# Attention and a mixture of experts on 4096 tokens: the results of three quarters of the tokens are summed and stored while experts still run

## The chip, the cores and the metric

The kernel runs on one core of one Trainium2 chip, as one launch. A core has five engines that run their own instruction streams side by side and wait for one another by semaphores: TensorE (PE in the profile, with its weight loads as PEld), VectorE (DVE), ScalarE (ACT), GpSimd (POOL) and SyncE (SP, which here only issues DMAs and reads small numbers). DMAs are issued into queues by SP, ACT and POOL and move data between DRAM and on-chip memory. The metric is the time of one execution in device microseconds (us); lower is better.

## The reference

The input is 16 sequences of 256 tokens with 128 channels, 4096 tokens in all. Cut to what matters:

```python
xn  = layernorm(x)
# attention: 16 heads of 8 channels, causal
Q, K, V = relu(xn @ Wq + bq), relu(xn @ Wk + bk), relu(xn @ Wv + bv)
attn = softmax(causal(Q @ K.T / sqrt(8)))          # per head
o    = attn @ V + xn
att  = gamma * (o - mean(o)) / sqrt(var(o) + eps) + beta
# mixture of experts: 8 experts, each token goes to its best two
h     = rms_weight * xn * rsqrt(mean(xn * xn) + eps)
top_w, top_i = top_k(softmax(h @ gate_w.T), 2)     # weights scaled to sum 1
moe   = xn + sum over the two: top_w * (silu(h @ w1.T) * (h @ w3.T)) @ w2.T   # 448 inner
out   = x + att + moe
```

Each of the eight experts has three matrices of 448 by 128. A token's result needs its attention and the results of two experts, whichever these are.

## The kernel before, in words

The 4096 tokens are 32 groups of 128 (one token per partition), in 8 blocks of 4 groups (`NB`, `BT`, 512 tokens: two sequences). Attention runs in 16 units, two per block: a unit `(n, r)` is block n with one half of the heads. Its parts are called `scores` (the products of queries and keys `S`, then VectorE's row maxima `tops`, lines 663 to 694), `queries` (`Qs`, `Qm`, line 705 on), `weights` (`W` and the exponentials `e`, lines 739 to 765, with causal masks on GpSimd), `values` (`O`, lines 780 and 791) and `finish` (transposes `o_ps`, `y`, and the statistics `mv`, lines 804 to 847).

Tokens are routed in three parts, `ROUTES`: groups 0 to 15, 16 to 23 and 24 to 31. `route` writes each token's row and weight into a DRAM list of its expert (GpSimd indirect DMAs, line 555). `planned` (line 856) turns the number of tokens per expert into a plan: which 256 rows of which expert each tile works on. The tiles come in three waves (9 possible after the first part, 17 after the second, the rest after the third; `WAVES`), and the plan goes through a wave expert by expert. 36 tiles are the usual count (`USUAL`); the up to three more stand behind a branch on the real count (line 1225).

`experts` (line 942) handles one tile after another. A tile is fetched two tiles ahead on SP's queue (its 256 rows `frows` and the three matrices, with 5, 3, 3 and 2 buffers), its rows are transposed (`hT`), and two halves of `A` and `G` (line 1000) give `hid` by way of ACT (line 1008) and VectorE (lines 1009 and 1011); `Y` (line 1017) is the down product. `deliver` transposes it back (`R_ps`, line 1031), adds the rows' own share on VectorE (`fres`, line 1033), and GpSimd scatters the rows with two indirect DMAs into `places`, a DRAM array with two rows for every token (line 1037). So a token's two expert results lie side by side in `places` once both of its tiles are delivered.

`rest` (line 1079) completes a pair of blocks on the attention side: SP loads x (line 1084, one buffer), GpSimd adds beta and x into `xn` (lines 1086, 1087), VectorE does a Newton square root on the statistics (`lv` at line 1090, `newton_sqrt` at 261 to 273, `nm` at line 1093), ACT scales `y` (line 1099), GpSimd multiplies by gamma and adds `xn` (lines 1100, 1101).

The order of TensorE's instructions is the order in which the program is written. Between the parts of a unit the program calls `fill` (line 1133), seven times per unit: each call adds an allowance for routing and planning, for exact masks and for the experts (1.57 expert steps, `EXPERT_STEPS`; a tile has four steps) and lets that much of each go on, and one step of `rest`. The other engines' orders, SP's and POOL's queues among them, are decided by a scheduler, which takes what is ready by its own reckoning of times; so an operation may stand far from its place in the program.

At the end, when all tiles are delivered, eight loads of 512 KB bring `places` back, one per block (`z`, line 1238, alternately in SP's and ACT's queue), VectorE adds the two rows to `y` (16 additions, line 1243), and eight stores of 256 KB write the output (line 1244):

## Time and profile before

| | |
|---|---|
| median of 10 runs | 701.37 us (699.7 to 703.02) |
| the profiled execution's own time | 702.03 us |
| its span in the profile | 700.1 us |
| TensorE busy, mean granted clock | 555.6 us (79%), 0.909 |
| VectorE / ScalarE / GpSimd busy | 470.6 / 321.4 / 271.7 us |
| DMA | 50.81 MB, mean 73 GB/s |
| 72 scatters of expert results (line 1037) | 72.4 us of GpSimd |
| 16 additions of `z` (line 1243) | from 684.0 us on; median 0.685 us of one |

Times in the profile count from the start of the span. The slices show in tenths how busy an engine was in each fortieth of the span (17.5 us). "PEclk" is the clock that TensorE was granted, 1.00 being full speed. In the time line a row is: start, length, engine, line, operation, output and inputs with their shape, and in brackets how long the engine stood idle before it and what it then waited for. The chain of waits is followed back from the last instruction; its rows are: start, length, what.

### The profile page before, as it was taken

The numbers are of one execution on the slowest core, as the hardware profiler recorded it, in microseconds if no ns is written. First come the engines' busy times: TensorE is split into PE (matmuls) and PEld (weight loads), VectorE is DVE, ScalarE is ACT, GpSimd is POOL, SyncE is SP. The second block draws the span as 40 slices with busy tenths as digits, with TensorE's granted clock in tenths as the row PEclk, the third lists the DMA queues.
The fourth block names the chain that finished last, engine by engine and source line by source line (L and its number), as shares of the span: only waits on it lengthen the run. The fifth ranks groups of instructions, "written<-read, shape, count | busy, mean of one in ns | idle before, by whom it ended". The sixth has DMA issues, their size and how long they took to land.

```text
span 700.1 us, 10306 instructions
## 1 busy us (share of the span) xinstructions
PE 555.6 (79%) x3280; PEld 330.9 (47%) x3293; DVE 470.6 (67%) x1287; ACT 321.4 (46%) x708; POOL 271.7 (39%) x401
## 2 busy tenths in 40 slices
PE   0267879597898919989799999889999998999830
PEld 0133434243565506555456555555566555556520
DVE  4956799854477934969558676968377649674356
ACT  2353466238434624354354545384454452835420
POOL 7600006880001572116733325264224235773451
PEclk9988879759899959999899999999999999999975
DMA  6000001115112322223332312332132312331019
GB/s 166 1 0 1 0 1 35 42 39 156 45 44 63 86 78 63 62 58 116 103 110 68 95 56 62 93 95 68 49 95 61 95 58 63 116 116 53 16 47 327
DMA packets 40760, 50.81 MB, mean 73 GB/s; under 512 B 5924, under 2 KB 33072, under 8 KB 40704
## 3 DMA queue, kind: packets, MB, share of 16 engines
q1 hardware_dynamic: 32128, 38.11, 18.6%
q0 software_dynamic: 4352, 8.47, 3.7%
q10 hardware_dynamic: 4224, 3.55, 1.6%
q8 instruction: 27, 0.44, 0.3%
q14 instruction: 29, 0.24, 0.1%
HBM read 38.35 MB, written 12.27 MB: 72 GB/s over the span
## 4 chain that ended last, share of the span: by engine, by line
PE 55%; DVE 26%; ACT 11%; DMA 4%; issue 2%; another core or an unknown queue 1%; POOL 0%; SPq 0%; DVEq 0%; ACTq 0%; POOLq 0%
PE S L663 8%; PE A L1000 8%; PE Y L1017 8%; PE G L1000 7%; PE W L739 6%; ACT e L762 4%; PE S L676 4%; PE O L780 4%; DVE tops L686 3%; DVE tops L694 3%; PE O L791 2%; PE q_ps L600 2%; ACT p L419 2%; DMA y<-in_x_dram 2%; DMA z<-places 2%
## 5 line engine op out<-in xcount | busy, mean ns | idle before, releaser
L1037 POOL DMA_INDIRECT places<-fres,frows x72 | 72.4, 1005 | 219.2 <-DVE fres L1033 149.3
L762 ACT ACTIVATE e<-W 128x512 f32<-128x512 f32 x192 | 99.9, 602 | 56.7 <-PE W L739 29.3
L1009 DVE SCALAR_TENSOR_TENSOR th<-th,A 112x512 f32<-112x512 f32 x72 | 49.2, 684 | 99.1 <-ACT th L1008 89.0
L694 DVE TENSOR_REDUCE tops<-S 128x2 f32<-128x512 f32 x128 | 79.6, 681 | 29.7 <-PE S L676 26.3
L1000 PE MATMUL A<-hT,w 128*112 128x256 f32 x288 | 78.8, 397 | 15.1 <-ACT hT L991 11.3
L765 POOL TENSOR_SCALAR_AFFINE_SELECT e<-e 128x256 f32<-128x256 f32 (+1 forms) x108 | 51.0, 496 | 79.2 <-ACT e L762 77.3
L663 PE MATMUL S<-KTm,QT 32*128 32x256 f32 (+1 forms) x512 | 76.9, 566 | 1.5 <-ACT e L762 1.5
L1000 PE MATMUL G<-hT,w 128*112 128x256 f32 x288 | 77.2, 392 | 0.0
L1017 PE MATMUL Y<-hid,w 112*128 112x256 f32 x288 | 72.2, 395 | 4.5 <-DVE Qs L712 2.1
L555 POOL DMA_INDIRECT lists<-rows_c,ratu_c x64 | 66.3, 1037 | 18.6 <-issue 16.7
L739 PE MATMUL W<-Qm,KT 32*128 32x512 f32 (+1 forms) x512 | 62.6, 544 | 3.0 <-ACT Qm L715 3.0
L1000 PEld LDWEIGHTS A<-hT,w 128*112 128x112 f32 x288 | 48.9, 182 | 33.2 <-ACT hT L991 14.9
L1017 PEld LDWEIGHTS Y<-hid,w 112*128 112x128 f32 x288 | 55.4, 197 | 18.7 <-issue 3.5
L1000 PEld LDWEIGHTS G<-hT,w 128*112 128x112 f32 x288 | 52.8, 183 | 12.2
L1008 ACT ACTIVATE th<-A 112x512 f32<-112x512 f32 x72 | 43.0, 597 | 32.7 <-PE A L1000 31.9
L801 ACT COPY oT<-O 128x512 f32<-128x512 f32 x32 | 18.7, 585 | 78.4 <-PE O L791 64.9
L1011 DVE TENSOR_TENSOR hid<-th,G 112x512 f32<-112x512 f32 x72 | 49.3, 685 | 7.4 <-PE O L791 1.7
L663 PEld LDWEIGHTS S<-KTm,QT 32*128 32x128 f32 x512 | 35.7, 200 | 22.1 <-issue 10.3
L780 PE MATMUL O<-e,vstat 128*32 128x512 f32 x256 | 39.0, 661 | 7.8 <-DVE Qs L712 4.4
L600 PE MATMUL q_ps<-xnT,wq_sb 128*128 128x512 f32 x32 | 22.4, 787 | 28.5 <-DVE Qs L712 22.7
L686 DVE TENSOR_REDUCE tops<-S 128x4 f32<-128x512 f32 x64 | 39.8, 681 | 4.6 <-PE S L676 4.5
L676 PE MATMUL S<-cmask,ident_bf 128*128 128x256 bf16 (+1 forms) x192 | 39.2, 330 | 0.0
(238 smaller groups left out, 860.3 us busy)
## 6 DMA issues: line engine op xcount, KB each, us to landing
w<-in_w1T_dram SPq DMA_DIRECT2D x36, 224.0 KB
w<-in_w3T_dram SPq DMA_DIRECT2D x36, 224.0 KB
w<-in_w2T_dram SPq DMA_DIRECT2D x36, 224.0 KB
frows<-lists SPq DMA_DIRECT2D x36, 130.0 KB
x<-in_x_dram SPq DMA_DIRECT2D x8, 256.0 KB
z<-places SPq DMA_DIRECT2D x4, 512.0 KB
z<-places ACTq DMA_DIRECT2D x4, 512.0 KB
lists<-filling SPq DMA_DIRECT2D x9, 130.0 KB
```

Of the source, the lines that this page charges most:

```text
L555: ins = G.indirect_dma_start(out=lists, out_offset=bass.IndirectOffsetOnAxis(ap=at_u[:, r, b + t : b + t + 1], axis=0), in_=rows[:, t, :], ...
L663: T.matmul(out, lhsT=QT[rows, q0 : q0 + P], rhs=KTm[rows, :, b * SEQ : b * SEQ + nk], start=(part < 2 or b == 0), stop=False, skip_group_c ...
L676: T.matmul(out, lhsT=ident_bf, rhs=cmask[:, 0, :].unsqueeze(1).to_broadcast([P, 4 if part == 2 else 2, P]), start=False, stop=True, skip_g ...
L686: ins = V.tensor_reduce(top[:, :, 0, cols], sp[g].rearrange("p (b j k) -> p b j k", b=2, j=HG), AX.X, ALU.max, negate=True,).ins
L694: ins = V.tensor_reduce(top[:, part, 1, cols], sp[g].rearrange("p (j k) -> p j k", j=HG), AX.X, ALU.max, negate=True,).ins
L739: T.matmul(out, lhsT=KT[rows, k0 : k0 + P], rhs=Qm[rows, :, k0 : (b + 1) * SEQ], start=(part > 0 or b == 0), stop=on_pool and (part > 0 or ...
L762: ins = S.activation(e[:, g, :], sp[g], AF.Exp).ins
L765: behind["POOL"] = G.affine_select(on, on, [[0, nd], [1, P]], ALU.is_ge, no_weight, base=0, channel_multiplier=-1).ins
L780: T.matmul(op[rows, :], lhsT=v[:, 2 * b, r * NG + g, :], rhs=e0[:, g, :], start=True, stop=False, skip_group_check=True, tile_position=(0, ...
L1000: T.matmul(to[:, ts(c, SL)], lhsT=wt[:, 0, ts(2 * k + c, CI)], rhs=hT, start=True, stop=True,)
L1017: T.matmul(yp, lhsT=w2[:, 0, c, :], rhs=hid[c // 2][:, ts(c % 2, SL)], start=(c == 0), stop=(c == NCI - 1),)
L1037: ins = G.indirect_dma_start(out=places, out_offset=bass.IndirectOffsetOnAxis(ap=rows[:, a, C : C + 1].bitcast(U32), axis=0), in_=res[:, a ...
```

## The change

`sums(pool, blocks)` takes the place of the final loop. For each block it loads `z` on SP, adds the two rows of `z` to each other and then adds `y` (two VectorE operations of 512 elements, into `z`), and stores `z` on SP. Loads run four blocks ahead of the additions (`LAG`), with six buffers in memory that the routing's pool has given back. It is called by `early_sums` from `fill` and from the last experts: blocks 0 to 3 begin once tile 26 is delivered in program order and the attention side of these blocks is complete, blocks 4 and 5 once tile 33 is (`READY`). Blocks 6 and 7 follow behind all experts.

This holds if the tiles that the first 16 groups need are among the first 26 in the plan, and those of the first 24 groups among the first 33. `planned` now orders a wave's tiles in turns over the experts (first tile of every expert, then the second, and so on) instead of expert by expert. It puts the pairs of expert and tile on partitions and gets each one's number from small TensorE products. The last wave's plan also counts the tiles that stand too late; if there are any, the sums and stores of blocks 0 to 5 are repeated at the very end, behind a branch.

`rest` for blocks 4 and 5 moves from behind all units into the last block's units. `EXPERT_STEPS` goes from 1.57 to 1.56. The DMAs that fill the lists' ends stand in another group of independent writes.

```diff
-    FIRST_US, EARLY_US, MASK_US, EXPERT_STEPS, EXPERTS_FROM = 4.0, 1.1, 0.7, 1.57, 3
+    FIRST_US, EARLY_US, MASK_US, EXPERT_STEPS, EXPERTS_FROM = 4.0, 1.1, 0.7, 1.56, 3
+    READY = [(16, 26), (24, 33)]
...
     def planned(w):
...
-        before = tiny("before", [P, E])
-        pair = norm.tile([P, E, E], F32, tag="pair", name=f"pair_{w}")
-        V.tensor_tensor(pair, earlier, left.unsqueeze(1).to_broadcast([P, E, E]), ALU.mult)
-        V.tensor_reduce(before, pair, AX.X, ALU.add)
...
+        there = tiny("there", [P, 1], BF16)
+        V.tensor_tensor(there, by_pair[:, 0:1], pair_j, ALU.is_gt)
...
+        yield PAUSE
+        op = misc(f"order_ps_{w}")[:, 0:1]
+        T.matmul(op, lhsT=behind_bf, rhs=there, start=True, stop=False)
+        T.matmul(op, lhsT=ones_bf, rhs=there, start=False, stop=True)
+        number = tiny("number", [P, 1])
+        V.scalar_tensor_tensor(number, there, -FAR, op, ALU.mult, ALU.add)
...
+        chosen = tiny("chosen", [P, 2, nk])
+        for k, of in ((0, pair_e), (1, row)):
+            V.tensor_scalar(
+                chosen[:, k, :], tile_no[:, 0:nk], number, of, ALU.is_equal, ALU.mult
+            )
...
+        yield PAUSE
+        cp = misc(f"plan_ps_{w}")[:, : 2 * nk]
+        T.matmul(
+            cp, lhsT=ones_f, rhs=chosen.rearrange("p a k -> p (a k)"), start=True, stop=True
+        )
...
+            wp = misc(f"worked_ps_{w}")[:, 0:E]
+            T.matmul(wp, lhsT=ones_bf, rhs=done, start=True, stop=True)
...
+        lp = misc(f"late_ps_{w}")[:, 0:NR2]
+        T.matmul(lp, lhsT=ones_bf, rhs=late_bf, start=True, stop=True)
+        late_i = tiny("late_i", [P, 1], I32)
+        V.tensor_reduce(late_i, lp, AX.X, ALU.max)
+        tiles_at["late"] = late_i
...
+    def sums(pool, blocks):
+        at = {}
+        for k in range(len(blocks) + LAG + 1):
+            if 0 <= k - LAG - 1 < len(blocks):
+                n = blocks[k - LAG - 1]
+                nc.sync.dma_start(out=ov[:, ts(n, BT), :], in_=at.pop(n)[:, :, 0, :])
+            if k < len(blocks):
+                n = blocks[k]
+                z = pool.tile([P, BT, 2, C], F32, tag="z", bufs=ZBUFS, name=f"z_{n}")
+                ins = nc.sync.dma_start(out=z, in_=pv[:, ts(n, BT)]).ins
+                tc.add_to_no_dep_group("places", ins)
+                at[n] = z
+            if 0 <= k - LAG < len(blocks):
+                n = blocks[k - LAG]
+                z = at[n]
+                V.tensor_tensor(z[:, :, 0, :], z[:, :, 0, :], z[:, :, 1, :], ALU.add)
+                V.tensor_tensor(z[:, :, 0, :], z[:, :, 0, :], y[:, ts(n, BT), :], ALU.add)
+            yield
+    LAG, ZBUFS = 4, 6
...
         beside(side["rest"])
+        early_sums()
+    last_pool = []
+    def early_sums():
+        if not last_pool:
+            if delivered[0] <= READY[0][1] or exact_upto[0] < NB or rested[0] < READY[0][0] // BT:
+                return
+            assert next(early_work, None) is None
+            early.__exit__(None, None, None)
+            last_pool.append(tc.tile_pool(name="last", bufs=1))
+            last_pool.append(last_pool[0].__enter__())
+            side["sums"] = sums(last_pool[1], range(READY[0][0] // BT))
+        if delivered[0] > READY[1][1] and rested[0] >= READY[1][0] // BT and not summed:
+            summed.append(True)
+            side["sums"] = chain(
+                side["sums"], sums(last_pool[1], range(READY[0][0] // BT, READY[1][0] // BT))
+            )
+        next(side["sums"], None)
...
-        if r == 0 and n % 2 == 0 and n >= 4:
+        if r == 0 and n in (4, 6, 7):
             for _ in side["rest"]:
                 pass
-            side["rest"] = rest(n - 4, n - 2, ffn_pool)
+            k = {4: 0, 6: 2, 7: 4}[n]
+            side["rest"] = rest(k, k + 2, ffn_pool)
...
-    side["rest"] = chain(rest(NB - 4, NB - 2, ffn_pool), rest(NB - 2, NB, ffn_pool))
+    side["rest"] = rest(NB - 2, NB, ffn_pool)
     for _ in side["experts"]:
         next(side["rest"], None)
+        early_sums()
...
-    early.__exit__(None, None, None)
-    late_pool.__exit__(None, None, None)
-    last = ctx.enter_context(tc.tile_pool(name="last", bufs=NB, reuse_waits="tile"))
-    for n in range(NB):
-        z = last.tile([P, BT, 2, C], F32, tag="z", name=f"z_{n}")
-        eng = nc.sync if n % 2 == 0 else nc.scalar
-        eng.dma_start(out=z, in_=pv[:, ts(n, BT)])
-        zs.append(z)
-    for n in range(NB):
-        yn = y[:, ts(n, BT), :]
-        for r in range(2):
-            V.tensor_tensor(yn, yn, zs[n][:, :, r, :], ALU.add)
-        (nc.sync if n % 2 == 0 else nc.scalar).dma_start(out=ov[:, ts(n, BT), :], in_=yn)
+    while len(summed) < 1:
+        early_sums()
+    for _ in side["sums"]:
+        pass
+    for _ in sums(last_pool[1], range(READY[1][0] // BT, NB)):
+        pass
+    with tc.If(number("late", P) > 0):
+        for _ in sums(last_pool[1], range(READY[1][0] // BT)):
+            pass
+    last_pool[0].__exit__(None, None, None)
```

## The prediction

> **What bounds the kernel now.** I read the page's busy table, slices and chain by engine first:
>
> ```profile
> span 700.1 us, 10306 instructions
> PE 555.6 (79%) x3280; PEld 330.9 (47%) x3293; DVE 470.6 (67%) x1287; ACT 321.4 (46%) x708; POOL 271.7 (39%) x401
> PE   0267879597898919989799999889999998999830
> DMA  6000001115112322223332312332132312331019
> PE 55%; DVE 26%; ACT 11%; DMA 4%; issue 2%; another core or an unknown queue 1%; POOL 0%; SPq 0%; DVEq 0%; ACTq 0%; POOLq 0%
> ```
>
> TensorE carries the kernel until the last two slices (8, 3, then 0); in the last one DMA is at 9. So an end without TensorE can be shortened, while in the middle whatever holds TensorE up costs its full length. Second, busy time by stretch (stretch, length, PE, PEld, DVE, ACT, POOL, granted clock, DMA share, GB/s), here 605 to 640 us and two pieces of the end:
>
> ```profile
> 605.00:640.00 35.00, 33.54 (x222) 20.78 (x218) 22.63 (x46) 18.41 (x39) 21.55 (x27) 1.00 0.31 89
> 665.00:680.00 15.00, 6.10 (x40) 3.95 (x32) 9.69 (x33) 3.29 (x8) 6.49 (x6) 0.84 0.05 16
> 680.00:700.00 20.00, 0.00 (x0) 0.00 (x0) 11.00 (x16) 1.64 (x5) 5.43 (x4) 0.50 0.92 315
> ```
>
> At 605 to 640 TensorE idles 1.5 us of 35, VectorE 12: extra VectorE work fits there only if TensorE need not wait for what stands behind it. After 680 DMA is 92% busy. Third, the chain of waits and the time line at the end:
>
> ```profile
> 677.15 2.13 DMA places<-fres,frows
> 679.49 4.38 DMA z<-places
> 686.92 6.17 DMA z<-places
> 695.75 0.69 DVE y L1243
> ...
> 678.02 0.17 DVE L1093 SCALAR_TENSOR_TENSOR nm<-mv,l_r 128x8 f32<-128x8 f32 x1
> 684.08 1.69 POOL L1101 TENSOR_TENSOR y<-y,xn 128x512 f32<-128x512 f32 x1
> 693.22 3.23 DVE L1243 TENSOR_TENSOR y<-y,z 128x512 f32<-128x512 f32 x5 [1.41 <-DMA z<-places]
> ```
>
> The last scatter's start releases eight loads of 512 KB 2.13 us later; they last until about 693, though `y` itself is complete at 684.08 + 1.69 = 685.8. Fourth, the time line at 577 to 586, the one place where VectorE, GpSimd and an x load collide late in the kernel, and its clock:
>
> ```profile
> 577.47 4.27 DVE L625 TENSOR_SCALAR KTm<-KT,head_mask 128x512 f32<-128x512 f32 x1
> 577.71 2.51 POOL L1086 TENSOR_TENSOR xn<-xn,beta_sb 128x512 f32<-128x512 f32 x2
> 582.74 1.88 PE L1000 MATMUL A<-hT,w 128*112 128x256 f32 x4 [1.81 <-DVE th L1009]
> 584.32 1.26 POOL L1087 TENSOR_TENSOR xn<-xn,x 128x512 f32<-128x512 f32 x1 [2.88 <-DMA x<-in_x_dram]
> ...
> 584.00:586.00 2.00, 2.00 (x6) 1.22 (x4) 1.86 (x7) 0.00 (x0) 1.26 (x1) 0.50 0.21 61
> ```
>
> A KTm that usually takes 0.48 lasts 4.27 us while GpSimd does beta and x adds. TensorE idles 1.81, and the granted clock then reads 0.50: the A and G groups take 1.88 and 1.91 instead of 1.03. That is 1.81 + 0.85 + 0.88 = 3.5 us for one VectorE delay of 3.8.
>
> **1. The tail.** Removed behind the last scatter: six of eight z loads, twelve of sixteen adds, six of eight stores; scatter-to-sum no longer sets the end. Next late is the normalising chain of the last eight groups. Before, `nm` ends at 678.2 and the last GpSimd operation at 685.8, that is nm + 7.6 (eight scales on ACT, then four GpSimd operations of 1.26 to 1.69). In the new order the last attention transposes stand one A/G group earlier on TensorE (before: "A1_35, o_ps, R34"; after: "o_ps, A1_35, R34"), worth 1.75, so the first tiny operation (`lv`) starts near 670.5 instead of 671.7. Its chain took 6.5 us and now shares VectorE with z4's and z5's four adds (0.70 each, 2.8): nm at 679.8. GpSimd ends at 687.4; one last add 0.7, issue 0.45, store to end 3.2 (before: 696.9 to 700.1), and a branch on the late flag, 0.3 (the scales of `y` on ACT around before's count branch took 1.50 for three instead of 0.43 each): 692.0. Against 700.1 that is -8.1. z6 and z7 are issued near 680 behind the last scatter and, at the 4.38 of the first z load above, land near 685.5, before `y`; if loads needed that row's 6.17 they would still tie. Unshown is how a z add beside GpSimd's operations stretches (one add took 1.64 instead of 0.69): 0 to 2.5 us more.
>
> **2. Sums among the experts.** z0 to z3: 2 MB of loads, eight adds, four stores, moved into 605 to 640. On SP the z loads wait for the scatters of tiles 28 and 29, and the fetches of 33 and 34 queue behind them; those are two tiles ahead of use (a tile takes about 9 us here), so a delay of 3 us is covered; without that cover a late tile costs its full delay. The outs wait on SP for the adds, with frows_34 and weights of 33 behind them, again under the same cover. VectorE has no cover. The four adds of z0, z1 stand ahead of the row maxima `tops` of the last unit's first scores, of fres29 and of tile 30's second half. Placed on the trace by hand: fres28 at 606.1, its scatter landed at 609.6, z0 and z1 landed near 613.1 (3.5 for 512 KB, between 2.85 of a 256 KB x load and 4.38); VectorE is ready at 610.4, ends the adds at 615.9 and `tops` at 618.4, and TensorE's weights of that unit start 2.8 late. For z2 the same count gives 3.7 late; z3 is landed by then. Stores add nothing to VectorE. Bounds: 0, if loads land before VectorE arrives, and 6.5 of idle plus twice 1.7 of slow clock, 9.9. The nearest row is the KTm block: a VectorE delay of 3.8 cost 3.5. Two such: I take +7.0.
>
> [...]
>
> **3. The rest work moved.** x adds and normalising of blocks 4 and 5 go from the end to the last block's units, those of 2 and 3 stand elsewhere against KTm. In the new GpSimd order beta and x adds of blocks 2 and 3 no longer lie where KTm of the last block runs, by a gap near 576.7 to 579.5 that it just fits: -3.5 (bounds -3.5 and 0). GpSimd now waits for block 5's x load, one buffer, ahead of a causal mask of the last unit: before, such a wait was 2.88 and 2.67 us; the mask has over 2 us of slack behind the late `tops` of step 2: +0.5 (0 to 2). The 17 tiny VectorE operations of the moved normalising (0.2 each, 3.5) leave the same engine earlier: 0 beside work that waits anyway, at worst 3.5 if `Qs` stands behind them.
>
> **4. Planning.** VectorE's planning instructions go from 74 to 66 of about 0.2 us, beside other work: 0, at worst 1.6 less or more. TensorE gets some 12 tiny matmuls, nearest the logit ones (64 in 8.2 us, 0.13 each): +1.6. They wait for VectorE with a pause between, which leaves whole work steps of cover; uncovered, a wait is one VectorE operation. The new tile order is the same 36 tiles of equal size: 0. EXPERT_STEPS 1.56 moves experts half a step later, already counted in 1. Counted with the inputs, the last tile that first-half tokens need is number 23 (of 26 allowed), and 31 (of 33) for the third quarter: the late flag stays 0 and the repetition does not run.
>
> Sum: -8.1 + 7.0 - 3.5 + 0.5 + 1.6 = **-2.5**. The profiled execution, 702.03 (its span 700.1 and 1.9 around it), is 0.66 above the median 701.37; from the median: **698.9**.
>
> **Rivals.**
> A, slower: one mechanism, the z adds at the head of VectorE's queue. If both waits come in full with the slow clock (9.9) and KTm is still stretched (0 for -3.5): -8.1 + 9.9 + 0.5 + 1.6 = +3.9, 705.3. It decides from the point where the waits cost over 6.0 with KTm unhelped, or 9.5 with it. For it: TensorE idles only 1.5 of 35 us there. Against: the last three tiles end with TensorE waiting on chains anyway, which can absorb some.
> B, loads hidden: the DMA share is 0.31 at 605 to 640, so z lands early and the waits cost 1: -8.1 + 1 - 3.5 + 0.5 + 1.6 = -8.5, 692.9. Against: a scatter-to-sum path of 7 us, and VectorE reaches the adds before.
> C, the tail keeps half: the z adds and GpSimd hold each other up, as in the KTm row, and the tail gains 4 only: +1.6, 703.0. Against: two tiny chains interleaved leave gaps.
> D, the repetition runs after all: 6 x 768 KB = 4.5 MB at the tail's 315 GB/s, about 15 us, with its own tail saved none: near 714. Only a wrong count would do it.
>
> **How the numbers follow.** My forecast .36, A .32, B .20, C .11, D .01. The trace also holds one TensorE idle stretch of 13.9 us (before 259.8) whose releaser the profile doesn't name; it can move with the order, which widens each case by a few us. The range reaches from under B, 690, to just past A, 706. About 0.2% (1.4 us) is what the measurement can tell from no change. Faster by more than that: B, most of the forecast, a little of C: .52. Within: .11. Slower: A, the rest of C, D: .37.
>
> **What would show it.** Step 1: one or two z loads behind the last scatter, end set by POOL's last `y` add, TensorE's last matmul to the span's end near 19 us instead of 27. Step 2: adds on VectorE at 610 to 630 with idle ended by "DMA z" of 2 to 4 us, PE idle before the last unit's W, and a granted clock below 1 behind it. Step 3: KTm of the last block at 0.5. Step 4: no second set of z loads. By the sum TensorE's last matmul ends near 678.3 (672.7 + 5.6); I am wrong if it ends before 675 or after 682.

## The result, and the profile after

| | before | after |
|---|---|---|
| median | 700.88 us of 40 runs (698.19 to 703.19) | 713.98 us of 11 runs (712.54 to 719.91) |
| profiled execution, its span | 702.03, 700.1 | 716.78, 714.5 |
| ratio of the times, 95% interval | | 1.0196 (1.018 to 1.0212) |

The changed kernel is 2.0% slower by the ratio of the times; the two medians alone give 1.9%. The forecast was 698.9 with a range of 690 to 706: wrong in sign, and the result lies outside the range. The profiled execution of after is 2.8 us above its median, that of before 1.1, so the spans below differ by 14.4 us where the medians differ by 13.1. The page of the changed kernel, the lines shown of before:

```profile
span 714.5 us, 10340 instructions
PE 568.6 (80%) x3295; PEld 337.5 (47%) x3308; DVE 457.1 (64%) x1279; ACT 322.0 (45%) x708; POOL 274.9 (38%) x403
PE   0267888497897867957999999989998999988870
DMA  6000001114112221222422321423223214353123
PE 54%; DVE 22%; ACT 12%; issue 5%; DMA 3%; another core or an unknown queue 2%; POOL 2%; DVEq 0%; POOLq 0%; ACTq 0%; SPq 0%
```

TensorE is busy 13 us longer for nearly the same work, and its slices 13 to 21 hold 7, 8, 6, 7, 9, 5, 7, 9, 9, where before has a single slice of 1 (the idle stretch of 13.9 us) and 7 to 9 otherwise. The end has lost the slice in which DMA is busy for 90% or more (9 before, 3 now). To see where the time went I cut both spans at the starts of attention's transposes `o_ps`, of which there are 32, one for each sequence and half of the heads:

| stage, cut at the n-th `o_ps` | before | after | difference |
|---|---|---|---|
| start to 8th | 218.3 | 221.2 | +2.9 |
| 8th to 14th (planning, list scatters) | 134.8 | 149.8 | **+15.0** |
| 14th to 26th | 215.1 | 210.1 | -5.0 |
| 26th to 28th (KTm of the last block) | 39.9 | 34.8 | -5.1 |
| 28th to 32nd (last unit, early sums) | 59.9 | 72.9 | **+13.0** |
| 32nd to the end | 32.2 | 25.7 | -6.5 |

Busy time by stretch (stretch, length, PE, PEld, DVE, ACT, POOL, granted clock, DMA share, GB/s): the two stages in bold, first of before, then of after, and of after the 35 us around the sums and the end too:

```profile
218.29:353.09 134.80, 108.81 (x660) 66.50 (x661) 92.09 (x261) 58.23 (x127) 57.28 (x72) 0.91 0.27 81
608.00:667.85 59.85, 56.09 (x349) 36.29 (x349) 31.80 (x71) 27.97 (x57) 30.42 (x42) 0.97 0.19 57
```

```profile
221.24:371.03 149.79, 117.25 (x670) 72.40 (x671) 89.73 (x252) 58.38 (x127) 59.43 (x72) 0.90 0.25 74
615.95:688.82 72.87, 62.84 (x350) 39.42 (x350) 40.17 (x97) 29.37 (x59) 36.89 (x47) 0.91 0.33 103
616.00:651.00 35.00, 31.41 (x169) 19.29 (x168) 24.26 (x57) 10.90 (x21) 13.94 (x17) 0.85 0.48 151
695.00:714.00 19.00, 0.18 (x2) 0.00 (x0) 8.47 (x23) 3.19 (x8) 9.31 (x8) 0.53 0.38 120
```

In the last unit TensorE runs the same 350 matmuls; it idles 10.0 us instead of 3.8 and is busy 6.8 longer at a lower granted clock (0.91 instead of 0.97). The planning stage is different: there VectorE does less than before, TensorE has ten more matmuls, and yet it idles 32.5 us instead of 26.0 and is busy 8.4 longer.

The time line of after around the first sums (start, length, engine, line, operation, and in brackets the idle time ahead of it and what ended it):

```profile
624.16 1.11 DVE L1193 TENSOR_TENSOR z<-z 128x512 f32<-128x512 f32 x1 [2.40 <-POOL e L771]
627.62 2.48 DVE L700 TENSOR_REDUCE tops<-S 128x2 f32<-128x512 f32 x4
628.36 3.86 PE L745 MATMUL W<-Qm,KT 32*128 32x512 f32 x8 [3.24 <-DVE tops L700]
632.15 2.05 PE L1066 MATMUL A<-hT,w 128*112 128x256 f32 x4
638.57 0.69 DVE L1193 TENSOR_TENSOR z<-z 128x512 f32<-128x512 f32 x1 [1.94 <-DMA z<-places]
```

This is step 2's picture: four additions ahead of `tops`, TensorE idle for 3.24 us before `W`, and then `W`, `A` at a granted clock of 0.50 from 628.4 to 634.2 (3.86 and 2.05 us; 1.14 and 1.03 before). The end of after, by the chain of waits (start, length, what) and by the time line:

```profile
698.91 2.44 DMA places<-fres,frows
701.42 3.68 DMA z<-places
705.12 1.48 DVE z L1193
706.72 1.54 DVE z L1194
```

```profile
694.75 0.44 PE L1097 MATMUL R_ps<-ident,yT 128*128 128x128 f32 x2 [0.52 <-DVE z L1193]
700.29 0.17 DVE L1160 SCALAR_TENSOR_TENSOR nm<-mv,l_r 128x8 f32<-128x8 f32 x1
706.12 1.59 POOL L1168 TENSOR_TENSOR y<-y,xn 128x512 f32<-128x512 f32 x1
709.00 0.69 DVE L1194 TENSOR_TENSOR z<-z,y 128x512 f32<-128x512 f32 x1
```

Two z loads are left behind the last scatter. They land at 705.1, before `y` is complete at 707.7, and TensorE's last matmul ends 19.3 us before the end: step 1 as forecast. The stretched KTm is gone; in after the last two blocks' KTm on VectorE read:

```profile
580.32 0.49 DVE L631 TENSOR_SCALAR KTm<-KT,head_mask 128x512 f32<-128x512 f32 x1 [2.79 <-issue]
591.25 0.47 DVE L631 TENSOR_SCALAR KTm<-KT,head_mask 128x512 f32<-128x512 f32 x1
```

What the prediction has no step for is the planning stage. At 306 to 327 us of after:

```profile
314.83 0.86 PE L797 MATMUL O<-e,vstat 128*32 128x256 f32 x8
325.31 0.58 ACT L807 COPY oT<-O 128x512 f32<-128x512 f32 x1 [9.45 <-remote]
325.95 0.69 PE L1097 MATMUL R_ps<-ident,yT 128*128 128x128 f32 x2 [9.89 <-issue]
```

ACT copies `O`, whose last matmul is recorded as ended at 315.7, only at 325.31. Its idle time is put down to "remote", that is, to no releaser that the profile shows. The 13.9 us stretch of before that the prediction named is of the same kind: VectorE waits 5.5 and 3.8 us for products that TensorE had long written (`o_ps` and `top_ps` are recorded as ended at 245.4 and 245.9), and TensorE's next instruction waits for `Qs`, which comes of the second. (TensorE's own row names `Qs`; it is VectorE's waits that have no releaser.)

```profile
254.82 0.17 DVE L813 TENSOR_SCALAR rs<-o_ps 128x16 f32<-128x16 f32 x1 [5.50 <-remote]
259.06 0.69 DVE L712 TENSOR_TENSOR Qs<-QT,top_ps 128x512 f32<-128x512 f32 x1 [3.77 <-remote]
259.80 2.08 PE L600 MATMUL q_ps<-xnT,wq_sb 128*128 128x512 f32 x2 [13.91 <-DVE Qs L712]
```

I call these late completions: a consumer starts late, in these two profiles 2 to 13 us after the recorded end of the matmul it needs, and the profile shows no releaser. All whose wait is over 2.5 us begin to wait within bursts of the routing's list scatters (`lists`, GpSimd: before 108 to 159, 240 to 262, 324 to 347; after 109 to 159, 246 to 269, 309 to 331). ACT and VectorE idle 20.7 us for "remote" in before, and ACT 27.2 in after; not all late completions are put down so, and the sum is no measure of what they cost.

One sentence of the description of the kernel has to be put right: `fres` does not add the rows' own share; it multiplies the tile's result by the router's weight.

### The profile page after: what moved, and what is told of

Its sections match the earlier page's. It is cut to its first block, busy times and chain, and to the rows that moved or that the text cites. A ratio compares the mean times of both kernels' runs of the same rounds, so it can differ in the third digit from the quotient of the medians.

```text
span 714.5 us, 10340 instructions
## 1 busy us (share of the span) xinstructions
PE 568.6 (80%) x3295; PEld 337.5 (47%) x3308; DVE 457.1 (64%) x1279; ACT 322.0 (45%) x708; POOL 274.9 (38%) x403
## 4 chain that ended last, share of the span: by engine, by line
PE 54%; DVE 22%; ACT 12%; issue 5%; DMA 3%; another core or an unknown queue 2%; POOL 2%; DVEq 0%; POOLq 0%; ACTq 0%; SPq 0%
PE Y L1083 8%; PE A L1066 7%; PE S L669 7%; PE G L1066 6%; PE W L745 6%; PE O L786 4%; ACT e L768 4%; PE S L682 4%; DVE tops L700 4%; PE O L797 2%; PE q_ps L606 2%; DVE tops L692 2%; DMA y<-in_x_dram 2%; ACT p L422 1%
## 5 line engine op out<-in xcount | busy, mean ns | idle before, releaser
L1103 POOL DMA_INDIRECT places<-fres,frows x72 | 73.9, 1026 | 226.2 <-DVE fres L1099 172.4
L1083 PE MATMUL Y<-hid,w 112*128 112x256 f32 x288 | 76.0, 409 | 16.3 <-DVE taken L517 4.6
L745 PE MATMUL W<-Qm,KT 32*128 32x512 f32 (+1 forms) x512 | 65.8, 559 | 5.7 <-DVE tops L700 3.2
L786 PE MATMUL O<-e,vstat 128*32 128x512 f32 x256 | 40.5, 676 | 7.7 <-DVE rs L827 7.2
L692 DVE TENSOR_REDUCE tops<-S 128x4 f32<-128x512 f32 x64 | 39.9, 681 | 5.4 <-PE S L682 5.4
L1091 ACT COPY yT<-Y 128x256 f32<-128x256 f32 x36 | 13.4, 372 | 57.8 <-PE Y L1083 57.7
```

Source lines behind the costliest of these rows:

```text
L692: ins = V.tensor_reduce(top[:, :, 0, cols], sp[g].rearrange("p (b j k) -> p b j k", b=2, j=HG), AX.X, ALU.max, negate=True,).ins
L745: T.matmul(out, lhsT=KT[rows, k0 : k0 + P], rhs=Qm[rows, :, k0 : (b + 1) * SEQ], start=(part > 0 or b == 0), stop=on_pool and (part > 0 or ...
L786: T.matmul(op[rows, :], lhsT=v[:, 2 * b, r * NG + g, :], rhs=e0[:, g, :], start=True, stop=False, skip_group_check=True, tile_position=(0, ...
L1083: T.matmul(yp, lhsT=w2[:, 0, c, :], rhs=hid[c // 2][:, ts(c % 2, SL)], start=(c == 0), stop=(c == NCI - 1),)
L1103: ins = G.indirect_dma_start(out=places, out_offset=bass.IndirectOffsetOnAxis(ap=rows[:, a, C : C + 1].bitcast(U32), axis=0), in_=res[:, a ...
```

## The experiments

Sixteen runs in four sets; each set ran on a chip of its own, beside runs of the kernel before on that chip. Four theories are named in the expectations:

- **P**: in the planning stage TensorE, in its written order, waits for VectorE's operands of the new small products.
- **L**: the bursts of list scatters stall TensorE, and how much depends on what happens to lie beside them.
- **S**: VectorE's additions of the early sums, waiting for their loads ahead of the row maxima, hold TensorE by more than was forecast.
- **C**: the late completions belong to the chip or the hour, and the change makes more of them.

### Set 1: one part of the change at a time

**Planning alone** (the kernel before with the new tile order and its products; no sums, old order of `rest`, 1.57 steps):

```diff
     def planned(w):
-        before = tiny("before", [P, E])
...
+        op = misc(f"order_ps_{w}")[:, 0:1]
+        T.matmul(op, lhsT=behind_bf, rhs=there, start=True, stop=False)
...
```

> The kernel before with only the new planning (pairs on partitions, turns over the experts, three pauses, twelve small TensorE products, count of late tiles which nothing reads); attention's rest, sums, tail and 1.57 as before. Theory P (the planning itself holds TensorE up): the 15 us that the changed kernel's TensorE is later at 371 us (18 late there, 3 late at 224) show here too, median 714 to 718. Theory L (the burst of list scatters stalls TensorE by an amount that depends on how the work falls beside it): the time moves by anything from -10 to +15, and the profile shows it as one or two idle stretches of TensorE of 4 to 14 us inside a burst, not as waits on the planning's own operations. My prediction's term: +1.6, 703.

Measured: 704.66, 1.0107 (1.0055 to 1.0158) of before (698.34 in this set). The stage from the 8th to the 14th `o_ps` takes 140.4 us, against 133.0 to 133.8 in the two kernels of this set that keep the old planning. So the new planning costs some 7 us here, as the ratio says too. Late completions ("remote") are there again: 17.9 us on ACT, 7.8 on VectorE.

**All sums at the end** (changed kernel, without sums among the experts):

```diff
         beside(side["rest"])
-        early_sums()
...
         next(side["rest"], None)
-        early_sums()
```

> The changed kernel without the calls that begin the sums early: all eight blocks are loaded, summed and stored behind the last expert, on SP alone with six buffers. Theory S (the early sums cost TensorE 13 us between 616 and 689, from which the tail gives back 7 to 9): the middle gets 13 faster, the tail 9 to 12 slower, so 709 to 714. If the early sums cost only the predicted 7: 715 to 719. If the 13 us were caused by something else: about 724.

Measured: 717.64, 1.0267 (1.0228 to 1.0306): the last unit falls to 63.9, 9.0 less than in the result, and the tail rises to 38.2, 12.5 more. The total lies where it was expected if the sums cost only 7; the stages say 9.0, and a tail that is dearer than the 9 to 12 expected. There all eight blocks go through six buffers, and loads and stores through one queue; no run separates which of these makes the tail so long. Without any sums 63.9 is still 4.0 above before's 59.9. Up to the sums TensorE's order is that of the changed kernel, and its planning stage takes 147.2 here, with 16.8 us of "remote" on ACT and 8.8 on VectorE.

**The moved `rest` alone:**

```diff
-        if r == 0 and n % 2 == 0 and n >= 4:
+        if r == 0 and n in (4, 6, 7):
...
-    side["rest"] = chain(rest(NB - 4, NB - 2, ffn_pool), rest(NB - 2, NB, ffn_pool))
+    side["rest"] = rest(NB - 2, NB, ffn_pool)
```

> The kernel before with only the rest of blocks 4 and 5 moved into the last block's units. By the prediction's step 3: -3.5 + 0.5 and a shorter tail chain hidden behind the z loads, 698 to 699. Theory L: nothing ahead of 560 us moves, so the stall near 246 to 260 stays as it is (13.9 us) and the change is within 3 us. If the KTm stretch is not removed: 701 to 703.

Measured: 698.3, 0.9992 (0.9966 to 1.0017). KTm's stage falls from 39.9 to 35.6, and the last unit rises from 59.9 to 63.6: -4.3 and +3.7. The move only shifts the price by one unit. What the price is made of stands in TensorE's rows, first of this run, then of before:

```profile
628.63 3.61 PE L1017 MATMUL Y<-hid,w 112*128 112x256 f32 x8 [2.58 <-DVE Qs L712]
```

```profile
632.89 1.99 PE L1017 MATMUL Y<-hid,w 112*128 112x256 f32 x8 [0.78 <-DVE Qs L712]
```

In this run the 17 tiny operations of the moved normalising, `lv` at 622.41 to `nm` at 627.46, run on VectorE ahead of `Qs` at 627.95; TensorE waits 1.8 us longer for `Qs` and then runs `Y` 1.6 us longer, at a granted clock of 0.55 from 628.6 to 632.3. (This profile puts 4.2 us down to "remote" in all, and its planning stage is 133.8 all the same. The stretch of 13.9 us is 11.6 here, though nothing ahead of 560 us was edited, so theory L's "stays as it is" missed.)

**1.56 alone:**

```diff
-... = 4.0, 1.1, 0.7, 1.57, 3
+... = 4.0, 1.1, 0.7, 1.56, 3
```

> The kernel before with only 1.56 for 1.57. Theory P: 700 to 702, since half an expert step moves nothing that matters. Theory L: the experts' steps fall otherwise beside the list scatters, TensorE's idle stretch of 13.9 us near 246 changes in length or place, and the time moves by more than 3 us.

Measured: 697.46, 0.9964 (0.9933 to 0.9996); the stage from the 14th to the 26th falls to 211.8 (214.8 in the run before it). The 2.5 us that the ratio stands for are neither P's standstill nor L's "more than 3".

### Set 2: the planning's waits, the steps, the place of the additions

**Two pauses instead of one** ahead of both groups of planning products:

```diff
         yield PAUSE
+        yield PAUSE
         op = misc(f"order_ps_{w}")[:, 0:1]
...
         yield PAUSE
+        yield PAUSE
         cp = misc(f"plan_ps_{w}")[:, : 2 * nk]
```

> The changed kernel with two pauses instead of one ahead of each pair of planning's TensorE products, so that TensorE reaches them one work step later. Theory P (TensorE waits in order for the planning's VectorE operands: 0.9, 1.4 and 4.4 us at 247 to 261 of the changed kernel's trace, 15 us in all between 221 and 371 with what follows from them): those waits vanish and 6 to 10 us come back, 704 to 708. Theory L (the loss there is the list scatters' stall, 9.9 and 4.3 us, placed by chance of the order): the planning waits vanish, but the time stays within 710 to 718 or jumps either way with other idle stretches.

**The changed kernel with 1.57 steps** (the line of the run above, back to 1.57):

> The changed kernel with 1.57 instead of 1.56. By itself 1.56 gave 2.5 us in the kernel before. Theory P: the change's loss stays, 714 to 717. Theory L (planning and 1.56 together put TensorE's work badly beside the list scatters; with 1.57 the new planning alone lost 7.5 us, and only 3 in its profiled execution): 704 to 710.

**Additions behind the end of the experts** (loads of blocks 0 to 5 stay among the experts, their additions follow `nm` of the last `rest`; eight buffers, stores in ACT's queue; the branch with the extra tiles moves behind these additions):

```diff
-    LAG, ZBUFS = 4, 6
+    ZBUFS = 8
...
+            with tc.issue_after(last_nm[0]) if behind_nm else ExitStack():
                 V.tensor_tensor(z[:, :, 0, :], z[:, :, 0, :], z[:, :, 1, :], ALU.add)
                 V.tensor_tensor(z[:, :, 0, :], z[:, :, 0, :], y[:, ts(n, BT), :], ALU.add)
-                nc.sync.dma_start(out=ov[:, ts(n, BT), :], in_=at.pop(n)[:, :, 0, :])
+            nc.scalar.dma_start(out=ov[:, ts(n, BT), :], in_=z[:, :, 0, :])
```

> The changed kernel with the six early z loads where they are, but their additions on VectorE behind the last normalising operation, and all stores in ACT's queue. Theory S (it is VectorE's z additions, waiting for their loads ahead of the last unit's row maxima, that hold TensorE up, 9 us between 616 and 679): that stage takes 54 us as without early sums instead of 63, and the end from the last transposes takes 26 to 29 instead of 25.1, so 706 to 709. If the loads themselves cost the 9 us (DMA queue, SP order, tile fetches late): 714 to 718.

**The same with the old planning** (tiles expert by expert again, loads from tiles 34 and 35 on, the late count on VectorE):

```diff
-    READY = [(16, 26), (24, 33)]
+    READY = [(16, 34), (24, 35)]
```

> A version built from the parts that paid: planning on VectorE alone as before, expert by expert, with the count of late tiles worked out by VectorE (ten tiny operations in the last wave), so blocks 0 to 3 may be loaded only when tile 33 is delivered and 4 and 5 when tile 34 is; additions behind the last normalising operation, stores in ACT's queue, rest of blocks 4 and 5 in the last block, 1.56. With no loss in the planning stage (133 us there), none from sums (54) and the shorter end (26 to 29 instead of 32): 690 to 695. If the loss at 221 to 371 is not the planning's: 700 to 710.

Measured, before at 685.16 on this chip:

| run | median | ratio (95%) | planning stage | 14th to 26th | last unit | tail |
|---|---|---|---|---|---|---|
| two pauses | 697.11 | 1.0187 (1.0131 to 1.0242) | 127.2 | 216.2 | 74.1 | 25.9 |
| 1.57 steps | 695.19 | 1.0158 (1.0097 to 1.022) | 130.1 | 213.3 | 77.6 | 27.3 |
| additions late | 680.44 | 0.9957 (0.9926 to 0.9988) | 126.3 | 210.1 | 63.2 | 28.2 |
| late, old planning | 681.6 | 0.9964 (0.9937 to 0.999) | 124.4 | 210.1 | 64.0 | 29.4 |

Two things follow. Before itself needs 15.7 us less than in the runs of the result, so that the expectations given in microseconds miss all four runs and only the ratios can be compared; and no profile of this set has a wait for "remote". And with the additions out of VectorE's way the changed kernel beats before, with the new planning or the old; between these two the planning stage differs by 1.9 us only. P falls where completions come in time: with twice the pauses the stage takes 127.2, no less than the 126.3 with one, and the experts move so that the next stage costs 216.2. With 1.57 steps the changed kernel is 1.6% slower than before though no completion is late; its last unit takes 77.6 (73.4 with 1.56 in set 3, one profile each), so what the sums cost seems to depend on where the experts' steps fall.

### Set 3: the changed kernel and before on one chip

No edit in the first two; the third is the kernel with late additions again.

> The kernel before, unchanged, for its profile on the same chip as the next three. Theory C (the idle stretches of TensorE inside the bursts of list scatters, whose completions come late, belong to the chip or the session: the profiles of the second set show none, and the kernel before ran 685 us there instead of 700): if this chip shows them, the stage from 218 to 353 us takes about 135 us and the span is near 700; if not, about 124 and 683.

> The changed kernel, unchanged, on the same chip as the kernel before's profile. Theory S+C: against that profile, the planning stage costs 2 to 3 us where no completion comes late and up to 15 where they do; the sum stage (last four groups of the attention's transposes before the end) costs 13, KTm gives 5, the end 7. So 1.005 to 1.012 on a chip without the late completions, 1.018 to 1.022 on one with them. Theory P (planning's waits are the larger part everywhere): 1.015 to 1.02 on either.

> The changed kernel with early loads, late additions and stores on ACT's queue, beside the changed kernel itself. Theory S: faster than the changed kernel by 7 to 11 us, all of it in the last unit and tiles 30 to 33, the stage before 570 us the same within 2. If it is 15 or more faster, part of that lies elsewhere and the profile says where.

**Additions spread** (as the third, but blocks 0 to 3 are added one at a time behind the weighing of tiles 31 to 34 and stored by SP; 4 and 5 behind `nm`):

```diff
+    SPREAD = {31: 0, 32: 1, 33: 2, 34: 3}
...
             delivered[0] = i + 1
+            if i in SPREAD and SPREAD[i] in loaded:
+                added([SPREAD[i]], weighed, nc.sync)
```

> Loads early as in the changed kernel, the additions of blocks 0 to 3 one block each behind the weighing of tiles 31 to 34's rows, where their loads landed long before, 4 and 5 behind the last normalising operation. Each block costs VectorE 1.4 us between experts. If no TensorE wait comes of them: the end is shorter than with all additions late (there VectorE's 16 additions end 6 us behind the last y) by 4 to 6 us, ratio 0.985 to 0.992. If VectorE's occupation alone, without any wait for a load, holds TensorE up: within 2 us of the kernel with all additions late.

Measured, before's runs beside at 685.79: before once more 686.32 (one profile); changed 688.65, 1.004 (1.0021 to 1.0058), just under the 1.005 to 1.012 expected; late additions 680.88, 0.9929 (0.9906 to 0.9952); spread 677.78, 0.9887 (0.9863 to 0.9912).

| stage | before | changed | late | spread |
|---|---|---|---|---|
| start to 8th | 215.6 | 215.1 | 215.5 | 212.1 |
| 8th to 14th | 121.8 | 126.4 | 126.4 | 129.3 |
| 14th to 26th | 214.8 | 210.1 | 210.1 | 210.1 |
| 26th to 28th | 40.0 | 34.8 | 34.8 | 34.8 |
| 28th to 32nd | 59.9 | 73.4 | 63.3 | 63.2 |
| 32nd to the end | 32.3 | 26.1 | 29.0 | 26.0 |

Here the change costs 0.4%, and every stage but the first two differs by the amount of the result's table to within 0.5 us. The last unit by stretch, before, changed and late:

```profile
592.25:652.10 59.85, 56.08 (x349) 36.25 (x348) 31.86 (x71) 28.05 (x57) 30.36 (x42) 0.97 0.20 57
```

```profile
586.42:659.77 73.35, 62.92 (x350) 40.45 (x349) 39.82 (x97) 29.40 (x59) 36.91 (x47) 0.93 0.33 102
```

```profile
586.86:650.13 63.27, 57.39 (x350) 36.92 (x350) 34.45 (x89) 29.03 (x59) 36.28 (x47) 0.97 0.32 101
```

The loads of z lie in this stage in both of the last two; the additions and the stores of blocks 0 to 3 (7.5 against 6.4 MB, rate times length) only in the changed kernel, and that is 10.1 us. With the additions spread, most of them and of the stores are in this stage again, the stores on SP as in the changed kernel, ahead of nothing that TensorE waits for, and cost it nothing (the stage takes 63.23 us against 63.27). So it is their place that costs the 10.1, and neither the additions nor the stores by themselves. The stage with the additions spread:

```profile
586.31:649.54 63.23, 57.36 (x350) 36.87 (x350) 39.00 (x95) 28.88 (x59) 36.70 (x45) 0.97 0.35 110
```

The changed kernel's time line, with the groups of TensorE that are affected, and the stretch behind the first of them:

```profile
595.04 0.73 DVE L1193 TENSOR_TENSOR z<-z 128x512 f32<-128x512 f32 x1 [2.80 <-DMA z<-places]
598.86 3.86 PE L745 MATMUL W<-Qm,KT 32*128 32x512 f32 x8 [3.27 <-DVE tops L700]
602.65 2.05 PE L1066 MATMUL A<-hT,w 128*112 128x256 f32 x4
609.16 0.69 DVE L1193 TENSOR_TENSOR z<-z 128x512 f32<-128x512 f32 x1 [2.32 <-DMA z<-places]
611.30 2.92 PE L669 MATMUL S<-KTm,QT 32*128 32x256 f32 x16 [0.37 <-DVE tops L700]
```

```profile
598.90:604.60 5.70, 5.70 (x13) 3.42 (x14) 3.22 (x6) 2.33 (x4) 2.49 (x4) 0.50 0.60 178
```

The same groups with late additions:

```profile
595.96 1.27 PE L745 MATMUL W<-Qm,KT 32*128 32x512 f32 x8
597.16 1.12 PE L1066 MATMUL A<-hT,w 128*112 128x256 f32 x4
604.35 1.17 PE L669 MATMUL S<-KTm,QT 32*128 32x256 f32 x16
```

Counted from the stage's start (586.42 and 586.86), `W` begins 3.3 us later than with late additions; at the clock of 0.50 `W`, `A` and `G` then take 3.86, 2.05 and 1.37 instead of 1.27, 1.12 and 1.03, another 3.8; and behind z2's wait the products `S` start 0.37 late and take 2.92 instead of 1.17, after which TensorE is 2.0 us further back. That is 9.1 of the 10.1; the rest falls where `Y` later waits 1.94 us for `Qs` instead of 1.03. S holds.

The late additions are dear elsewhere: six microseconds of them stand behind the last `y`. Time line at the end, in set 2's run:

```profile
664.28 1.59 POOL L1170 TENSOR_TENSOR y<-y,xn 128x512 f32<-128x512 f32 x1
670.55 1.28 DVE L1193 TENSOR_TENSOR z<-z,y 128x512 f32<-128x512 f32 x2
```

and with the additions spread:

```profile
633.53 1.42 DVE L1194 TENSOR_TENSOR z<-z 128x512 f32<-128x512 f32 x1
667.11 1.26 POOL L1172 TENSOR_TENSOR y<-y,xn 128x512 f32<-128x512 f32 x1
670.47 0.69 DVE L1195 TENSOR_TENSOR z<-z,y 128x512 f32<-128x512 f32 x1
```

Spread, the last addition ends 2.8 us behind `y` instead of 6.0, and no addition waits for a load among the experts. This version beats both kernels.

### Set 4: once more on another chip, and bursts broken up

> The kernel before, unchanged, for its profile beside the next three. If the late completions are there (stage 218 to 353 us near 135, span near 700) the three below tell what they do to the change; if not (124, near 685), they repeat the second same-chip comparison.

> The changed kernel, unchanged. Theory C: 1.018 to 1.022 where the profile of the kernel before shows late completions, with about 10 us more of them than before; 1.002 to 1.006 where it shows none. If it is 1.018 or more without late completions, theory C falls.

**List scatters spaced** (the changed kernel, with a pause behind every four list scatters of the second and third part):

```diff
+                if t0 and not (b + BT >= nt and r == 1):
+                    yield PAUSE
```

> The changed kernel with a pause after every four list scatters of the second and third route, so that a burst of 16 becomes four of 4, one per work step. Where completions come late: if it is the burst that makes them late, they go and 10 to 20 us come back against the changed kernel; if they only fall in the same time, they stay. Where none come late: the plans come some 20 us later, within 5 us of the changed kernel.

The spread additions again:

> The version with early loads and additions spread behind the rows of tiles 31 to 34, on this chip: 0.985 to 0.991 where no completion comes late; where they do, it has the changed kernel's planning and order up to 590 us, loses 10 us more to them than the kernel before, and comes out at 1.000 to 1.008.

Measured, before beside at 686.43: before once more 686.28; changed 688.78, 1.0038 (1.0013 to 1.0062); scatters spaced 694.64, 1.011 (1.0073 to 1.0148), 5.9 us behind the changed kernel where at most 5 were expected; spread 680.15, 0.99 (0.987 to 0.9929). Again no profile has a wait for "remote". So the spaced scatters could not show what they do to late completions; where there are none they only cost: the stage from the 14th to the 26th takes 216.2, as with more pauses. This set also shows how far one kernel's stages differ from one profile to the next: the changed kernel's planning stage takes 129.5 here and 126.4 in set 3, and the spread kernel's stage from the 14th to the 26th 213.2 here and 210.1 there. Differences of some 3 us between single profiles in these two stages are therefore not put down to an edit below.

### What the sets say of the late completions

The same kernel before takes 700.9 us in the runs of the result and 698.3 in set 1, and every profile from these runs has late completions (set 1 has none of before itself); it takes 685.2 to 686.4 in sets 2 to 4, with none in any of twelve profiles. By stretch, the planning stage of before and of changed in set 3:

```profile
215.61:337.42 121.81, 106.12 (x662) 65.35 (x660) 90.84 (x261) 58.10 (x127) 56.91 (x72) 0.96 0.32 89
```

```profile
215.09:341.47 126.38, 111.14 (x673) 68.09 (x671) 88.17 (x252) 58.43 (x127) 58.90 (x72) 0.96 0.31 87
```

Against these the result's profiles lose 13.0 us of 134.8 in before and 23.4 of 149.8 in after, the granted clock falling from 0.96 to 0.91 and 0.90; at the start they lose 2.7 and 6.1. So of the +14.4 between the result's spans, 1.5 is what the change costs where completions come in time, and 13.8 is more loss in the first two stages, less 0.9 of small differences in the other four. By set 4, where changed takes 129.5 in the planning stage and before 121.9, the excess is 11.6.

Much of the loss lies in a few gaps of TensorE. The 13.91 us ahead of `q_ps` in before are 4.40 in set 3. In after there are three such gaps, the last of them the 9.89 us ahead of `R_ps` shown above, and 0.34 in set 3. The rows are those of before in set 3, of after, and of changed in set 3:

```profile
247.61 2.08 PE L600 MATMUL q_ps<-xnT,wq_sb 128*128 128x512 f32 x2 [4.40 <-DVE Qs L712]
```

```profile
257.21 2.44 DVE L479 TENSOR_TENSOR rgt_c<-rgt_c,req_c 128x256 f32<-128x256 f32 x1
261.08 0.61 PE L959 MATMUL plan_ps<-chosen,ones_f 128*128 128x16 f32 x2 [4.37 <-DVE Qs L718]
274.42 3.78 PE L1083 MATMUL Y<-hid,w 112*128 112x256 f32 x8 [4.33 <-ACT oT L807]
```

```profile
300.40 0.44 PE L1097 MATMUL R_ps<-ident,yT 128*128 128x128 f32 x2 [0.34 <-ACT oT L807]
```

The second and third gap of after wait for `oT`, whose own wait is put down to "remote" (6.41 and 9.45 us). The first is another thing: VectorE's operation at 257.21 takes 2.44 us there and 0.42 in set 3, while GpSimd builds `rows_c`, and `Qs` comes late behind it; TensorE waits for `Qs`, not for the planning's `chosen`, which was written by 251.1. In set 3 the first of these gaps is 0.94 us and the second does not exist.

What makes completions late in some sets stays open; chip and time change together from set to set, and the chip of the result isn't on record. So does why the changed kernel suffers more. C's second half fits set 1 as well: with late completions the new planning in the old order takes 140.4, the changed kernel's order takes 147.2 there and 149.8 in the result, and old planning 133 to 134. Some half of the excess then goes with the new planning and half with the order around it, by one or two profiles each; which operation carries it isn't settled. L as a property of the bursts falls, since the same bursts run without such a stall in sets 2 to 4; that the place of other work beside them sets the amount where they do stall could not be tried.

## Why the prediction was wrong, step by step

All steps on one chip without late completions (set 3, changed less before, by stages) and in the result:

| step | predicted | set 3 | result |
|---|---|---|---|
| 1, the tail | -8.1 | -6.2 | -6.5 |
| 2, sums among the experts | +7.0 | +10.1 | together with the next +13.0 |
| 3, GpSimd and small VectorE work in the last unit | +0.5 | +3.4 | |
| 3, KTm | -3.5 | -5.2 | -5.1 |
| 4, planning, order, 1.56 | +1.6 | -0.6 | +12.9 |
| sum | -2.5 | +1.5 | +14.3 (spans: +14.4) |

**Step 1 was right.** Of its -8.1, 1.75 lies ahead of the cut at the 32nd `o_ps`, which stands one A/G group earlier in the new order; that leaves -6.35 for the stage, against -6.2 and -6.5. From TensorE's last matmul to the end it is 27.4 in before and 19.7 in changed, -7.7; "near 19 us instead of 27" was the forecast. The end is a near tie of loads and `y`, also as forecast.

**Step 2 had the mechanism and mis-sized it**, and with a term that step 3 put at nothing it turned the sign. The term "a VectorE delay of 3.8 cost 3.5. Two such" took both waits to cost what the KTm block cost. The first cost 7.1 (3.3 late, 3.8 of slower groups), as its idle time of 3.27 was followed by at least 5.7 us at a clock of 0.50; `W` took 3.86 there, three times the 1.27 with late additions; four `tops` run one after another ahead of it and beside it (598.12 to 600.60), and no run separates their part from the clock's. The second cost 2.0, with no slow clock behind it (1.00 from 606 to 618 us). The upper bound of 9.9 (idle plus slow clock) was 0.2 too low. Behind the gap of 3.24 us in the result the clock reads 0.50 too, as it does behind the gap of 1.81 us in before that the prediction shows.

**Step 3: the gain was right, the price was not.** KTm gives 4.3 to 5.2 back. The term that failed is the one for the 17 tiny VectorE operations, "0 beside work that waits anyway, at worst 3.5 if `Qs` stands behind them": in the run with the move alone `Qs` does stand behind them, TensorE waits 2.58 us for it instead of 0.78 and then runs slower, and the last unit costs 3.7 more, so that the move alone is worth nothing (0.9992). The wait for the mask that the +0.5 stood for is small there: 0.66 us ahead of `O`. The table's +3.4 is what the last unit costs beyond the additions; it is net of the 1.75 above, and holds the loads of z and the order as well, which no run separates.

**Step 4's products are not contradicted where completions come in time, and its zero for 1.56 left something out.** With the old planning and 1.56 the stage takes 124.4, with the new 126.3 (set 2): +1.9 for the forecast +1.6, but one kernel's stage differs by 3.1 between two profiles, so this is no more than agreement. What 1.56 does there isn't shown either. In the kernel before 1.56 alone gave 2.5 us by the ratio (0.9964), and the stage from the 14th to the 26th fell by some 3; in the changed kernel it is 210.1 with 1.56 and 213.3 with 1.57, though the spread kernel had 210.1 and 213.2 with 1.56 both times. "EXPERT_STEPS 1.56 moves experts half a step later, already counted in 1" looked at the end alone.

**What failed in the result as measured** is the sentence behind the chances, that the idle stretch of 13.9 us "can move with the order, which widens each case by a few us". It is one of several that go with a loss of some 16 us in before and 27 to 30 in after, by the comparison above. The prediction saw one stretch without a releaser and priced its movement at a few; with 12 to 14 us more of such loss no case of the forecast could hold. That D's "near 714" is the number measured is luck: its mechanism did not occur.

**The rivals.** A named its own point of decision, waits over 9.5 with KTm helped. They cost 10.1: on a chip without late completions it was A that came true, at +0.4%, and its 705.3 is 0.6% above the median it started from. B fell (2.80 and 2.32 us of waits for z, against loads landing early), C fell (the tail kept its gain), D did not happen: z is loaded eight times, not fourteen.

**The signs named beforehand.** TensorE's last matmul was to end within 675 to 682, 5.6 later than before; it ended at 695.2, and in set 3 at 666.2 against 657.0, 9.2 later. The other signs (two loads at the end, idle of 2 to 4 us ended by z, a slow clock behind `W`, KTm at 0.5, no second set of loads) came, the idle times in set 3; in the result they are 2.40 us, ended by GpSimd's `e`, and 1.94.

## What to carry to other kernels

An addition that waits for a load belongs behind work that VectorE has anyway, one block at a time, and not ahead of the operand that TensorE needs next: with the same loads the same additions cost 10.1 us in one place and next to nothing in another (63.23 us for the last unit with most of them in it, 63.27 with none), and the version with them spread is 1.1 and 1.0% faster than before on two chips, instead of 0.4% slower (where completions come late it was not run). A price that is moved to the next unit has to be asked for there, operand by operand; `rest` gave 4.3 and took 3.7, as tiny operations came to stand ahead of `Qs`. And where a trace holds idle time whose releaser it doesn't show, look at how much of it there is in all, since it can grow with a change: here the loss that goes with it was some 16 us in before and 27 to 30 in after.

## What the runs showed of the hardware that I had not expected

- In the profiles of the result and of set 1, consumers of TensorE's products wait for a releaser that the profile doesn't show; in the result's two they start 2 to 13 us after the recorded ends, and all such waits over 2.5 us begin within bursts of GpSimd's indirect list scatters. In the twelve profiles of sets 2 to 4, on three chips, no such wait is recorded. For the kernel before that goes with 698 to 701 against 685 to 686 us, and for the change with +2.0% against +0.4%.
- An idle gap of TensorE of 3.27 us was followed by at least 5.7 us at a granted clock of 0.50 (the changed kernel in set 3).
- A 512-element addition of the sums on VectorE, 0.68 to 0.69 us in after's medians, took 1.48 and 1.54 us at the end of after, while GpSimd worked on `y` (the chain's z rows above).
- The stage from the 14th to the 26th `o_ps` takes 210.1 to 216.2 us with the same work in it. One more pause, in the planning or between list scatters, goes with 216.2, steps of 1.56 and 1.57 mostly with 210.1 to 211.8 and 213.3 to 215.1; but one kernel took 210.1 and 213.2 in two profiles.
